# Cross attention on one core: in the first batch, Wv's sums and the next batch's A sums change places in VectorE's order

## Chip, core and metric

The kernel runs on one core of one Trainium2 chip. The metric is device time in microseconds (us). PE is the matrix engine, DVE the vector engine, ACT the scalar engine, POOL is GpSimd, and SP issues most transfers. "The trace" is one profiled execution of the kernel.

## What is computed

For eight batches, with x1 and x2 of 512 x 1024 (channels by positions), all in f32:

```python
q = jnp.einsum('bcn,dc->bnd', x1, Wq) + bq            # Wq 64 x 512
k = jnp.einsum('bcn,dc->bdn', x2, Wk) + bk[:, None]   # Wk 64 x 512
v = jnp.einsum('bcn,dc->bdn', x2, Wv) + bv[:, None]   # Wv 512 x 512
attn = jax.nn.softmax(jnp.einsum('bnd,bdm->bnm', q, k), axis=2)
attn_out = jnp.einsum('bcm,bnm->bcn', v, attn)
return attn_out + x1
```

## The kernel before

The product with v is reassociated: first y = x2 times the transposed attention (the "y" stage), then Wv times y (the "o" stage), plus bv and x1. Both are products of 2 x 2 blocks, and each is done with seven block products instead of eight (a Winograd form of Strassen's scheme). The left operand is A (x2 transposed, blocks "11" to "22") in the y stage and Wv (tiles `w`) in the o stage; its sums S1 to S4 are made by `left_sums`, four DVE instructions, of 128x1024 for A (through `sum_a`) and of 128x512 for Wv. The sum S3 is written over block 21. Wv's sums are made once, A's once per batch. The right operand, the exponentials e in the y stage and y in the o stage, has sums T1 to T4 (`sum_e`, `sum_y`).

The seven block products of a stage are numbered 1, 2, 6, 7, 5, 3, 4 as `multiply` knows them; the code's `first(i)` is a product of the y stage and `second(i)` one of the o stage. The y stage runs them in the order 1, 2, 6, 5, 7, 3, 4, with the next batch's scores before 5 and before 4; the o stage in the order 1, 6, 2, 5, 7, 3, 4 (the texts call these its stages). Products 1, 6, 5 and 3 accumulate in bank a, products 2, 7 and 4 in bank c; each bank has two halves (a0, a1; c0, c1), one per 128 rows. Products 1, 7 and 2 open a bank anew. After 1, 6 and 5 ACT copies the bank aside. The blocks of the result come out in the order 11, 22, 12, 21: 12 is read from bank a after product 3, the others from bank c.

Softmax runs on the scores transposed: `scores` (PE) and a copy to SBUF (ACT); `fold` takes the maximum over tiles (DVE); `highest` finishes it across partitions (POOL, tile `top`); `exponentials` subtracts it (DVE, L230) and exponentiates (ACT, L231). `sums` and `total` do the same with sums (tile `den`), and `shares` takes the reciprocal (DVE, L219).

The order is written out by hand. Each engine takes its instructions in the order of the code and stops at the first one whose inputs or buffers are not ready. `period(s, n, nn, nnn)` writes the work of batch s, and in between the scores and exponentials of the next batch n and the queries and keys of batches after it. `period` for s.b == 0 is the first batch. Lines to follow:

- L180 scores; the third tile of the second half goes to bank a (tile `ps_sa`), which `evict_y(s, "12")` (L306) must have emptied.
- L279 all block products of both stages (`ps_ya`, `ps_yc` for y; `ps_oa`, `ps_oc` for o).
- L308, L310 the evictions of y11, y22 and y21; L306 that of y12.
- L324, L331 the evictions of the result, `evict_o`; L332 their output transfers (SP).
- L100 the sums of `left_sums`, for A (`aS`, `a`) and for Wv (`w_S`, `w`).
- L201, L205 the folds; L210 and L215 POOL's reductions; L236 the T sums.
- L138 the projections of queries and keys (`ps_q`, `ps_k`).

Of the kernel before, what the change touches and what calls it, by code (L numbers as in the profile page):

```python
# [15 lines left out]
def kernel(  # L16
# [64 lines left out]
    w = {  # L81
        k: const.tile([P, 2, C // 2], F32, name=f"w_{k}")
        for k in ("11", "12", "21", "22", "S1", "S2", "S4")
    }
# [6 lines left out]
    def left_sums(a, *ks):  # L91

        for k in ks:
            x, y, op = {
                "S1": ("21", "22", ALU.add),
                "S2": ("S1", "11", ALU.subtract),
                "S3": ("11", "21", ALU.subtract),
                "S4": ("12", "S2", ALU.subtract),
            }[k]
            nc.vector.tensor_tensor(a["21" if k == "S3" else k], a[x], a[y], op)  # L100
            if k == "S3":
                a["S3"] = a["21"]
# [8 lines left out]
    def load_x(s, x):  # L111

        s.x = sb.tile([P, CT, N], F32, tag="x", name=f"x_{s.b}_{x.tensor.name}")
        for c in range(CT):
            nc.sync.dma_start(s.x[:, c, :], x[s.b, ts(c, P), :])

    def load_a(s, *ks):
        for k in ks:
            s.a[k] = sb.tile(
                [P, MH, C // 2], F32, tag=f"a{k}", name=f"a{k}_{s.b}", bufs=1 + (k[0] == "2")  # L120
            )
            nc.sync.dma_start(s.a[k], x2T[s.b, int(k[0]) - 1, int(k[1]) - 1])

    def sum_a(s, *ks):
        for k in ks:
            if k != "S3":
                s.a[k] = sb.tile([P, MH, C // 2], F32, tag=f"a{k}", name=f"a{k}_{s.b}")
        left_sums(s.a, *ks)
# [18 lines left out]
    def queries(s):  # L147

        ps = project(s, "q", wq_sb)
        s.q = sb.tile([P, N], F32, tag="q", name=f"q_{s.b}", bufs=2)  # L150
        for h, r, o in ((0, lo, hi), (1, hi, lo)):
            nc.scalar.activation(
                s.q[r, ts(h, H)], ps[r, :], AF.Identity, bias=bq_sb[r, :]
            )
        for h, r, o in ((0, lo, hi), (1, hi, lo)):
            nc.scalar.dma_start(s.q[o, ts(h, H)], s.q[r, ts(h, H)])

    def keys(s, bank=None):

        ps = project(s, "k", wk_sb, bank)  # L160
        s.k = sb.tile([P, H], F32, tag="k", name=f"k_{s.b}", bufs=2)
        nc.scalar.activation(s.k, ps, AF.Identity, bias=bk_sb)  # L162
# [49 lines left out]
    def total(s, h):  # L212
        fold_halves(s, h, ALU.add)
        s.den[h] = sb.tile([P, H], F32, tag="den", name=f"den_{s.b}_{h}", bufs=3)
        nc.gpsimd.partition_all_reduce(s.den[h], s.mx[h][:, 0, :], P, ReduceOp.add)  # L215

    def shares(s, h):
        s.rden[h] = s.den[h]
        nc.vector.reciprocal(s.rden[h], s.den[h])  # L219
# [18 lines left out]
    def open_t(s):  # L238
        for n in ("T1", "T2", "T4"):
            s.t[n] = sb.tile([P, MH, H], F32, tag=f"e{n}", name=f"e{n}_{s.b}")  # L240
        e0, e1 = s.e[0], s.e[1]
        s.t |= {"11": e0[:, 0], "12": e1[:, 0], "21": e0[:, 1], "22": e1[:, 1]}
        s.t["T3"] = s.t["12"]

    def sum_e(s, *ks):
        for i in (0, 2):
            part = {n: v[:, i : i + 2, :] for n, v in s.t.items()}
            for k in ks:
                right_sums(part, k)
# [19 lines left out]
    def multiply(s, stage, i, left, right, n_k):  # L269

        ka, kb, bank, opens = MULT[i]
        for j in range(2):
            if opens:
                s.bank[bank, j] = ps_a.tile(
                    [P, H], F32, tag=f"{bank}{j}", name=f"ps_{stage}{bank}{j}_{s.b}_{i}"
                )
            ps = s.bank[bank, j]
            for k in range(n_k):
                nc.tensor.matmul(  # L279
                    ps,  # L280
                    left[ka][:, k, ts(j, P)],
                    right[kb][:, k, :],
                    start=opens and k == 0,
                    stop=i in (2, 3, 4) and k == n_k - 1,
                    skip_group_check=True,
                )
            if i in (1, 6, 5):
                s.tmp[i, j] = sb.tile([P, H], F32, tag=f"u{i}{j}", name=f"u{stage}{i}{j}_{s.b}")
                nc.scalar.copy(s.tmp[i, j], ps)  # L289
# [29 lines left out]
    def evict_o(s, k):  # L319
        bank, add = RESULT[k]  # L320
        for j in range(2):
            c = 2 * (int(k[0]) - 1) + j
            o = s.o[k, j]
            nc.vector.scalar_tensor_tensor(  # L324
                o, s.bank[bank, j], bv_sb[:, c : c + 1], o, ALU.add, ALU.add
            )
        for j in range(2):
            c, h = 2 * (int(k[0]) - 1) + j, int(k[1]) - 1
            o = s.o[k, j]
            if add is not None:  # L330
                nc.vector.tensor_tensor(o, o, s.tmp[add, j], ALU.add)  # L331
            nc.sync.dma_start(out[s.b, ts(c, P), ts(h, H)], o)  # L332

    def sums(s, h):
        for i in range(1, MH):
            fold(s, h, i, "sum", ALU.add)
        total(s, h)
# [70 lines left out]
    def head_second(s, n):  # L408


        scores(s, 1, 3)()
        for i in range(2, MH):
            fold(s, 1, i, "max", ALU.max)
        queries(n)
        load_x(n, x2)
        highest(s, 1)
        sum_a(s, "S3", "S4")
        for i in range(MH):
            exponentials(s, 1, i)
# [11 lines left out]
    def period(s, n, nn, nnn):  # L431

        def first(i):
            multiply(s, "y", i, s.a, s.t, MH)

        def second(i):
            multiply(s, "o", i, w, s.y, 2)

        open_t(s)
        first(1)
        if s.b == 0:
            head_second(s, n)
        sum_e(s, "T1", "T2")
        if s.b == 0:
            total(s, 0)
        else:
            sum_e(s, "T4")
        if n:  # L450
            load_a(n, "11")
        first(2)
        if s.b == 0:
            keys(n)
            load_x(nn, x1)
            evict_y(s, "11", (1,))
            sum_e(s, "T4")
            shares(s, 0)
            evict_y(s, "11", (2,))
        else:  # L460
            shares(s, 0)
            evict_y(s, "11")
        sums(s, 1)
        sum_e(s, "T3")
        shares(s, 1)
        if n:
            load_a(n, "12", "21", "22")
        first(6)

        def next_queries():  # L470
            queries(nn)
            load_x(nn, x2)

        def next_keys():
            keys(nn)
            if nnn:
                load_x(nnn, x1)

        if n:
            scores_and(n, 0, "c", next_queries if nn else nothing)  # L480
            for i in range(1, MH):
                fold(n, 0, i, "max", ALU.max)
            highest(n, 0)
            if s.b == 0:
                left_sums(w, "S1", "S2", "S3", "S4")
        first(5)
        fetch_o(s, "11")
        fetch_o(s, "22")
        if n:
            for i in range(MH):  # L490
                exponentials(n, 0, i)
            if s.b:
                sum_a(n, "S1", "S2", "S3")
        first(7)
        evict_y(s, "22")
        first(3)
        evict_y(s, "12")
        if n:
            scores_and(n, 1, "a", next_keys if nn else nothing)
            sums(n, 0)  # L500
        sum_y(s, "T1")
        sum_y(s, "T2")
        if n:
            sum_a(n, *(("S4",) if s.b else ("S1", "S2", "S3", "S4")))
            for i in range(1, MH):
                fold(n, 1, i, "max", ALU.max)
            highest(n, 1)
        first(4)
        evict_y(s, "21")
        second(1)  # L510
        sum_y(s, "T3")
        sum_y(s, "T4")
        second(6)
        fetch_o(s, "12")
        if n:
            exponentials(n, 1, 0)
            exponentials(n, 1, 1)
        second(2)
        evict_o(s, "11")
        fetch_o(s, "21")  # L520
        second(5)
        if n:
            exponentials(n, 1, 2)
            exponentials(n, 1, 3)
        second(7)
        evict_o(s, "22")
        if n:
            second(3)
            evict_o(s, "12")
            second(4)  # L530
            evict_o(s, "21")
        else:
            second(4)
            evict_o(s, "21")
            second(3)
            evict_o(s, "12")
# [37 lines left out]
```

## Time and profile before

| | |
|---|---|
| median of 3 runs | 718.07 us (718.0 to 718.2) |
| the profiled execution | 718.06 us, of which the span is 716.0 us |
| PE busy | 706.1 us, 99% of the span |
| DVE busy | 590.9 us, 83% |
| ACT, POOL busy | 201.3 us (28%), 97.5 us (14%) |
| DMA | 87.39 MB, mean 122 GB/s |
| granted PE clock | 1.000 |

A busy PE is counted with overlapping instructions, so its share hides slow stretches; distances between the starts of stages show them. One batch follows another at 86.93 us once the kernel is under way (the first y product starts at 124.96 us in the second batch and at 211.89 us in the third). A wait of an engine is counted as idle time, with the instruction that ended it.

### The profile page before, as it was taken

To read this page: it belongs to the slowest core of one execution; us is meant where nothing else is said; L and a number is where in the kernel's file an instruction comes from. 1 tells how busy PE (TensorE), PEld (TensorE's weight loads), DVE (VectorE), ACT (ScalarE), POOL (GpSimd) and SP (SyncE) were. 2 spreads that over 40 slices of the span, in tenths; PEclk is the share of its full clock that TensorE was granted. 3 is DMA by queue.
4 is the path that set the end of the run, shared out by engine and by line. 5 is a ranking of instruction groups with operands and counts; after the bars stand their busy time and mean duration, and the time that the engine had idled before them with its cause. 6 is when DMAs were issued, how large, how long until landed. Compare 5 with 4: busy or idle time off the path is not lost.

```text
span 716.0 us, 5409 instructions
## 1 busy us (share of the span) xinstructions
PE 706.1 (99%) x1892; PEld 299.9 (42%) x1892; DVE 590.9 (83%) x569; ACT 201.3 (28%) x271; POOL 97.5 (14%) x38
## 2 busy tenths in 40 slices
PE   8999999999999999999999999999999999999997
PEld 4333334434444444444444443443434444444443
DVE  0999998988969888798887987889887898989444
ACT  2733313044210532215221232403324034230010
POOL 0132130030300311011200202002020020301000
PEclk9999999999999999999999999999999999999999
DMA  8577133341333503435133352332601350042004
GB/s 335 208 232 261 66 146 118 121 143 74 146 129 136 169 22 146 148 118 190 42 134 117 119 191 92 112 119 89 220 0 60 117 177 0 0 159 77 0 1 147
DMA packets 34699, 87.39 MB, mean 122 GB/s; under 512 B 3952, under 2 KB 3952, under 8 KB 34672
## 3 DMA queue, kind: packets, MB, share of 16 engines
q1 hardware_dynamic: 33344, 84.95, 33.8%
q10 hardware_dynamic: 1264, 2.10, 1.0%
q8 instruction: 15, 0.25, 0.1%
q14 instruction: 12, 0.10, 0.0%
q0 software_dynamic: 64, 0.00, 0.0%
HBM read 68.42 MB, written 16.78 MB: 119 GB/s over the span
## 4 chain that ended last, share of the span: by engine, by line
PE 85%; DVE 10%; DMA 2%; issue 1%; ACT 1%; SPq 0%; DVEq 0%; ACTq 0%
PE ps_ya L279 27%; PE ps_yc L279 20%; PE ps_oa L279 14%; PE ps_oc L279 12%; PE ps_s L180 5%; PE ps_k L138 3%; PE ps_q L138 3%; DVE max L201 2%; DMA a<-in_x2T_dram 1%; DVE e L230 1%; DVE eT L236 1%; DMA w<-in_wvT_dram 1%; DVE aS L100 1%; DVE den L219 1%; PE ps_sa L180 1%
## 5 line engine op out<-in xcount | busy, mean ns | idle before, releaser
L215 POOL PARTITION_ALL_REDUCE den<-sum x16 | 65.3, 4079 | 431.8 <-DVE sum L205 431.8
L279 PE MATMUL ps_ya<-eT,aS 128*128 128x512 f32 x256 | 113.1, 595 | 0.0
L279 PE MATMUL ps_yc<-e,a 128*128 128x512 f32 x256 | 112.6, 592 | 0.0
L289 ACT COPY uy<-ps_ya 128x512 f32<-128x512 f32 x48 | 28.1, 588 | 231.2 <-PE ps_ya L279 231.2
L230 DVE TENSOR_TENSOR e<-e,top 128x1024 f32<-128x1024 f32 x60 | 69.9, 1217 | 11.9 <-POOL top L210 11.9
L279 PEld LDWEIGHTS ps_ya<-eT,aS 128*128 128x128 f32 x256 | 48.0, 190 | 63.8 <-issue 63.5
L279 PEld LDWEIGHTS ps_yc<-e,a 128*128 128x128 f32 x256 | 48.6, 190 | 61.6 <-issue 60.1
L324 DVE SCALAR_TENSOR_TENSOR o<-ps_oc,bv_sb,o 128x512 f32<-128x512 f32 x48 | 35.8, 749 | 42.1 <-PE ps_oc L279 42.0
L231 ACT ACTIVATE e<-e 128x1024 f32<-128x1024 f32 x60 | 62.2, 1056 | 26.5 <-DVE e L230 24.7
L289 ACT COPY uo<-ps_oa 128x512 f32<-128x512 f32 x48 | 28.1, 585 | 131.0 <-PE ps_oa L279 127.7
L189 ACT COPY e<-ps_s 128x1024 f32<-128x1024 f32 x47 | 46.7, 1026 | 60.6 <-PE ps_s L180 60.6
L279 PE MATMUL ps_oc<-y,w 128*128 128x512 f32 x128 | 57.6, 593 | 0.3 <-DVE y L310 0.3
L279 PE MATMUL ps_oa<-yT,w_S 128*128 128x512 f32 x128 | 57.5, 592 | 0.0
L279 PE MATMUL ps_ya<-e,a 128*128 128x512 f32 x128 | 56.3, 593 | 0.8 <-ACT e L225 0.8
L279 PE MATMUL ps_yc<-eT,a 128*128 128x512 f32 x128 | 57.0, 598 | 0.0
L279 PE MATMUL ps_ya<-e,aS 128*128 128x512 f32 x128 | 56.2, 592 | 0.0
L219 DVE RECIPROCAL den<-den 128x512 f32<-128x512 f32 x16 | 53.6, 3348 | 0.0
L180 PE MATMUL ps_s<-q,k 64*128 64x512 f32 x188 | 47.9, 608 | 1.6 <-ACT k L162 0.8
L210 POOL PARTITION_ALL_REDUCE top<-max x16 | 30.6, 1913 | 133.6 <-DVE max L205 133.6
L308 DVE TENSOR_TENSOR y<-ps_yc,uy 128x512 f32<-128x512 f32 x48 | 31.2, 675 | 15.9 <-PE ps_yc L279 15.9
L201 DVE TENSOR_TENSOR max<-max,e 128x1024 f32<-128x1024 f32 x32 | 39.2, 1225 | 3.7 <-ACT e L187 0.5
L201 DVE TENSOR_TENSOR sum<-sum,e 128x1024 f32<-128x1024 f32 x32 | 39.2, 1225 | 2.1
(65 smaller groups left out, 758.6 us busy)
## 6 DMA issues: line engine op xcount, KB each, us to landing
x_in_x_dram<-in_x_dram SPq DMA_DIRECT2D x56, 512.0 KB, 5.6
a<-in_x2T_dram SPq DMA_DIRECT2D x32, 512.0 KB, 4.7
o<-in_x_dram SPq DMA_DIRECT2D x64, 256.0 KB, 6.4
out_dram<-o SPq DMA_DIRECT2D x64, 256.0 KB, 2.1
x_head<-in_x_dram SPq DMA_DIRECT2D x8, 512.0 KB, 8.0
q<-q ACTq DMA_DIRECT2D x14, 128.0 KB, 7.2
w<-in_wvT_dram SPq DMA_DIRECT2D x4, 256.0 KB, 8.9
wqk_sb<-in_wqk_dram ACTq DMA_DIRECT2D x1, 256.0 KB, 4.6
```

The source lines that it names most:

```text
L138: nc.tensor.matmul(ps[r, :], w_sb[:, c, :], s.x[:, c, ts(h, H)], start=(c == 0), stop=(c == CT - 1),)
L180: nc.tensor.matmul(ps[g], s.k[r, ts(i, P)], s.q[r, ts(h, H)], start=True, stop=True)
L189: nc.scalar.copy(e[:, :, i, :], whole)
L201: nc.vector.tensor_tensor(f, e[:, :, 0, :] if i == 1 else f, new, op)
L215: nc.gpsimd.partition_all_reduce(s.den[h], s.mx[h][:, 0, :], P, ReduceOp.add)
L219: nc.vector.reciprocal(s.rden[h], s.den[h])
L230: nc.vector.tensor_tensor(e, e, top, ALU.subtract)
L231: nc.scalar.activation(e, e, AF.Exp)
L279: nc.tensor.matmul(ps, left[ka][:, k, ts(j, P)], right[kb][:, k, :], start=opens and k == 0, stop=i in (2, 3, 4) and k == n_k - 1, skip_gr ...
L289: nc.scalar.copy(s.tmp[i, j], ps)
L308: nc.vector.tensor_tensor(y[:, j, :], ps, s.tmp[add, j], ALU.add)
L324: nc.vector.scalar_tensor_tensor(o, s.bank[bank, j], bv_sb[:, c : c + 1], o, ALU.add, ALU.add)
```

## The change

In the first batch only, two groups of DVE instructions get new places. The sums of Wv stood behind the maximum of the next batch's first half of scores; they now stand behind the sum T2 of y, where the next batch's A sums stood. Those A sums now stand behind the eviction of block 22 of the result, ahead of the evictions of 12 and 21. All other batches keep their order, and nothing is added or left out.

```diff
@@ -481,8 +481,6 @@
             for i in range(1, MH):
                 fold(n, 0, i, "max", ALU.max)
             highest(n, 0)
-            if s.b == 0:
-                left_sums(w, "S1", "S2", "S3", "S4")
         first(5)
         fetch_o(s, "11")
         fetch_o(s, "22")
@@ -501,7 +499,10 @@
         sum_y(s, "T1")
         sum_y(s, "T2")
         if n:
-            sum_a(n, *(("S4",) if s.b else ("S1", "S2", "S3", "S4")))
+            if s.b:
+                sum_a(n, "S4")
+            else:
+                left_sums(w, "S1", "S2", "S3", "S4")
             for i in range(1, MH):
                 fold(n, 1, i, "max", ALU.max)
             highest(n, 1)
@@ -524,6 +525,8 @@
             exponentials(n, 1, 3)
         second(7)
         evict_o(s, "22")
+        if s.b == 0:
+            sum_a(n, "S1", "S2", "S3", "S4")
         if n:
             second(3)
             evict_o(s, "12")
```

## The prediction

> **What bounds the kernel now.** I read the page's first part, then what PE waited for, then the timelines of PE, DVE and POOL through the first batch and the second beside it.
>
> ```profile
> span 716.0 us, 5409 instructions
> ...
> PE 706.1 (99%) x1892; PEld 299.9 (42%) x1892; DVE 590.9 (83%) x569; ACT 201.3 (28%) x271; POOL 97.5 (14%) x38
> ```
>
> PE is the bound almost throughout, so DVE work counts only where PE stands still for it. After the head of the kernel PE does that in two places, both in the first batch (columns: total us, times, longest us):
>
> ```profile
> PE ps_sa L180 <- DVE y L306: 1.4, 1, 1.4
> ...
> PE ps_oc L279 <- DVE y L310: 0.3, 1, 0.3
> ```
>
> The first is the third score tile of the second batch: it goes into bank a, which DVE has not yet emptied of y12. The second is stage 2 of the output, which needs y21. DVE's timeline shows what lay ahead of y12 (start, length):
>
> ```profile
> 75.74 0.69 DVE L205 TENSOR_TENSOR max<-max 128x512 f32<-128x512 f32 x1
> 76.35 0.69 DVE L100 TENSOR_TENSOR w_S<-w,w 128x512 f32<-128x512 f32 x1
> 77.07 1.41 DVE L100 TENSOR_TENSOR w_S<-w_S,w 128x512 f32<-128x512 f32 x1
> 78.41 0.68 DVE L100 TENSOR_TENSOR w<-w,w 128x512 f32<-128x512 f32 x1
> 79.01 0.68 DVE L100 TENSOR_TENSOR w_S<-w,w_S 128x512 f32<-128x512 f32 x1
> 79.61 4.62 DVE L230 TENSOR_TENSOR e<-e,top 128x1024 f32<-128x1024 f32 x4
> ...
> 86.55 1.27 DVE L306 TENSOR_TENSOR y<-ps_ya,den 128x512 f32<-128x512 f32 x2
> ```
>
> The four sums of Wv stand between the folded maximum and the exponentials, while POOL forms the maximum that the exponentials need. POOL's timeline, first batch and second:
>
> ```profile
> 76.61 2.07 POOL L210 PARTITION_ALL_REDUCE top<-max  x1 [8.03 <-DVE max L205]
> ...
> 157.47 1.78 POOL L210 PARTITION_ALL_REDUCE top<-max  x1 [8.02 <-DVE max L205]
> ```
>
> PE's timeline of the two batches gives the price of the waits, as distances between starts:
>
> ```profile
> 83.92 1.99 PE L180 MATMUL ps_s<-q,k 64*128 64x512 f32 x8
> ...
> 89.79 3.65 PE L138 MATMUL ps_k<-x_in_x_dram,wqk_sb 128*64 128x512 f32 x16
> ...
> 103.78 3.60 PE L279 MATMUL ps_oa<-yT,w_S 128*128 128x512 f32 x8
> 107.69 3.70 PE L279 MATMUL ps_oc<-y,w 128*128 128x512 f32 x8 [0.31 <-DVE y L310]
> ...
> 114.66 3.60 PE L279 MATMUL ps_oc<-y,w 128*128 128x512 f32 x8
> ...
> 124.96 7.03 PE L279 MATMUL ps_ya<-e,a 128*128 128x512 f32 x16
> ...
> 201.59 3.60 PE L279 MATMUL ps_oc<-y,w 128*128 128x512 f32 x8
> ```
>
> From the first score to the key projection takes 89.79 - 83.92 = 5.87 us here; in the second batch (173.67 to 177.30) it takes 3.63. So the wait costs 2.24 us, more than its 1.38 us of idle, because the second half of bank a is late too. From stage 6 to stage 7 takes 114.66 - 103.78 = 10.88; in the second batch (191.29 to 201.59) 10.30. That wait costs 0.58 us.
>
> **The change, part by part.** It only reorders eight DVE instructions. No operation, byte or DMA is added.
>
> *1. Wv's sums leave the place behind the maximum.* DVE gives back 79.61 - 76.35 = 3.26 us there, but the exponentials cannot start until POOL delivers the maximum. POOL starts at 76.61 and took 2.07 us with the sums beside it; in the second batch, with DVE idle, it took 1.78. The Trainium skill (SBUF — State Buffer, Who interferes with whom) says that a DVE instruction with two SBUF inputs contends with a GpSimd one that reads SBUF, and that whoever starts first holds the port for the whole instruction. The row of 1.41 us, a sum that otherwise takes 0.69, fits a collision, though not one held to the full 2.07. By the rule the reduction alone falls back to 1.78 and ends at 78.39; if its 2.07 is its own, it ends at 78.68. With the 0.04 us that DVE needs after it in the second batch (159.25 to 159.29) the exponentials start at 78.43 or 78.72, and DVE is 1.18 or 0.89 us earlier. I take 1.18: of the 16 maxima 13 have 1.78, and the three longer ones all have sums of DVE beside them.
>
> The y22 and y12 evictions follow straight behind, so bank a's halves come free 1.18 us earlier (the first at 86.06 instead of 87.24). PE cannot use them before 83.92 + 1.82 = 85.74, the distance that the second batch shows (173.67 to 175.49), so the whole 1.18 is on the path. About 1.06 of the 2.24 us stays lost. ACT's copies, which follow PE's scores by 1.17 us in the second batch, are not in the way.
>
> *2. Behind T2 of y, four sums of Wv stand in place of four sums of the next A.*
>
> ```profile
> 96.58 1.21 DVE L100 TENSOR_TENSOR aS<-a,a 128x1024 f32<-128x1024 f32 x1
> ...
> 101.24 1.22 DVE L201 TENSOR_TENSOR max<-e 128x1024 f32<-128x1024 f32 x1
> ```
>
> The A sums take 101.24 - 96.58 = 4.66 us. Those of Wv without the collision take 0.72 + 3 x 0.60 = 2.5 (the starts above; 0.72 where one needs the result just before it). DVE gains a further 2.1 and is then 3.3 us early; y21 is done about 3.3 us earlier, PE reaches it only 1.2 us earlier, and the 0.58 us of stage 2 goes. The sums' own users stay served: PE's stage 6 needs S2, due at about 96.7 against PE's 102.6; the others are needed later. Should one collide with POOL it costs 0.7 us more; y21's first half is due at 104.3 and PE wants it at 106.0, so 1.7 us of spare cover that, and I cost it at nothing. POOL's sum reduction (92.43 to 96.56, then 1.18 earlier) is over when they begin: T2 in front of them (3.15 us) ends with it.
>
> PE at stage 7 is then 1.18 + 0.58 = 1.76 us early: 112.90 instead of 114.66.
>
> *3. The A sums go behind the eviction of block 22.* Waiting behind them in DVE's queue are the evictions of 12 and 21, and in SP's queue their four output DMAs and the next load of A. The first product of the second batch needs bank a, which the eviction of 12 empties. From the second batch, where the end of stage 7 sets the pace:
>
> ```profile
> 207.09 0.74 DVE L324 SCALAR_TENSOR_TENSOR o<-ps_oa,bv_sb,o 128x512 f32<-128x512 f32 x1
> ...
> 211.89 7.03 PE L279 MATMUL ps_ya<-e,a 128*128 128x512 f32 x16
> ```
>
> Stage 7 starts at 201.59, so DVE reaches the eviction of 12 after 5.50 us and PE reaches the next batch after 10.30. Now 4.66 us of sums come between: the eviction starts after 10.16, its first half ends after 10.91 (0.75), and PE goes on 0.04 later (as from 87.24 to 87.28). So PE waits to 10.95 instead of 10.30: 0.65 us. The slack there, 10.30 - 5.50 - 0.75 - 0.04 = 4.01 us, covers most of the sums but not all. Bank a's second half is free 0.7 us later and needed 3.4 later.
>
> What is late next: the evictions of 12 and 21 take 1.33 + 1.33 + 1.20 = 3.86 us by their rows, so DVE begins the T sums of the second batch at 112.90 + 10.16 + 3.86 = 126.9 (127.03 now). PE is then 1.1 us early and DVE 0.1. They next meet at y11, where DVE now waits 0.99 us for PE at 138.96; that wait vanishes and nothing on PE moves. The SP queue holds no load that PE is near: the A load waits for PE's first product (131.82 now) with or without the change.
>
> Sum: -1.18 - 0.58 + 0.65 = -1.11 us; with about 0.05 for PE's restart (after the wait at 107.69 the next stage began 0.09 late) -1.06. From the second batch on no PE wait is recorded, so it reaches the end. The profiled execution took 718.06 us, 716.0 span and 2.06 around it, against the median 718.07: 718.07 - 1.06 = 717.0. Bounds: -1.3 if the bank wait is 0.4; -0.5 if the reduction stays at 2.07 and each A sum costs 0.06 more. The alternative by the port rule's absence alone is 0.29 higher, 717.3.
>
> **The rivals.**
>
> *The new wait does not form.* Then -1.76: 716.3, just over 0.2%. It needs the four sums done in 4.01 us, or bank a's first half free otherwise. For it: the margin is 0.65 us of 4.66, and PE's ends are modelled. Against it: DVE's queue is in order, the rows of the A sums hardly vary, and the last eviction of block 22 is tied to the end of stage 7, so DVE's earlier lead cannot be used. A milder form, a wait of 0.3, gives -1.4, at the 0.2% bound (1.44 us). 0.28 for more than 0.2%.
>
> *The A sums stall in their new place, and the second batch starts late.* Rows of collided A sums exist: the longest two took 1.94 and 2.06 us instead of 1.22. Four such take about 8.0 us, the wait at bank a becomes 4.0, and the balance is -1.76 + 4.0 = +2.2: 720.3. It decides from 1.76 + 4.01 = 5.8 us of sums to be slower at all, and from 7.2 to be slower by 0.2%. Against it: POOL has nothing between about 107.8 and 145.3, and both long rows lie beside a reduction in the head. 0.11, with unseen delays of that size at this place.
>
> *The first part does nothing*, because POOL or ACT holds the scores as late as before: then only 0.58 is gained and 0.65 lost, 718.1. The second batch, whose scores run without a wait, speaks against it. It lies within 0.2%.
>
> **How the numbers follow.** A measurement of this kernel can tell about 0.2% (1.44 us) from no change. My main case, -0.5 to -1.4, and the third rival lie within it: together 0.61. The range goes from the first rival, with 0.1 below it (716.2), to the third rival with 0.1 above (718.2); what is left out is nearly all of the slower case and a few hundredths of the others.
>
> **What would show it.** Right: POOL's reduction at 76.6 takes 1.78 us; the exponentials start at 78.4; PE waits for y12 0.3 to 0.5 us instead of 1.4; the wait for y21 is gone; a new PE wait of 0.5 to 0.8 us of ps_ya for the o of L324 near 123.8; the second batch's first product starts at 123.8 to 124.0. Wrong: that start at 123.2 (no wait), or after 125 (A sums stalled), or PE waits in the second batch, which I expect to have none.

## The result and the profile after

The changed kernel takes 717.1 us (median of 22 runs, 716.92 to 719.06), the kernel before 718.19 us in the same comparison (22 runs, 717.92 to 719.92). The ratio is 0.9986, 95% interval 0.998 to 0.9992: about 1.1 us, or 0.14%, faster, which lies within the 0.2% of the prediction. The forecast was 717.0 us.

PE's waits after (total us, times, longest us):

```profile
PE ps_ya L279 <- DVE o L324: 0.5, 1, 0.5
...
PE ps_sa L180 <- DVE y L306: 0.2, 1, 0.2
```

The wait for y12 fell from 1.4 to 0.2 us, the wait for y21 is gone, and there is one new wait: the first product of the second batch for the eviction of 12 (L324). DVE's timeline after (start, length):

```profile
75.58 0.69 DVE L205 TENSOR_TENSOR max<-max 128x512 f32<-128x512 f32 x1
78.26 4.63 DVE L230 TENSOR_TENSOR e<-e,top 128x1024 f32<-128x1024 f32 x4 [2.00 <-POOL top L210]
...
95.25 0.68 DVE L100 TENSOR_TENSOR w_S<-w,w 128x512 f32<-128x512 f32 x1
...
97.78 1.22 DVE L201 TENSOR_TENSOR max<-e 128x1024 f32<-128x1024 f32 x1
...
118.25 1.22 DVE L100 TENSOR_TENSOR aS<-a,a 128x1024 f32<-128x1024 f32 x1
...
122.92 1.40 DVE L324 SCALAR_TENSOR_TENSOR o<-ps_oa,bv_sb,o 128x512 f32<-128x512 f32 x2
```

This execution runs 0.16 us ahead of the one before already at the fold of 75.58 (75.74 before) and at the first score (83.76, 83.92 before). That arises at the head of the kernel, ahead of the first instruction that the change moves; distances between starts leave it out. From the fold to the exponentials DVE now takes 2.68 us instead of 3.87, and 2.00 of it is idle time that POOL ends. Wv's sums take 2.53 us behind T2, A's 4.67 us behind the eviction of 22. POOL's and PE's timelines after:

```profile
76.44 1.78 POOL L210 PARTITION_ALL_REDUCE top<-max  x1 [8.03 <-DVE max L205]
```

```profile
83.76 1.99 PE L180 MATMUL ps_s<-q,k 64*128 64x512 f32 x8
...
88.46 3.65 PE L138 MATMUL ps_k<-x_in_x_dram,wqk_sb 128*64 128x512 f32 x16
...
102.45 3.60 PE L279 MATMUL ps_oa<-yT,w_S 128*128 128x512 f32 x8
...
112.75 3.60 PE L279 MATMUL ps_oc<-y,w 128*128 128x512 f32 x8
...
123.72 7.13 PE L279 MATMUL ps_ya<-e,a 128*128 128x512 f32 x16 [0.51 <-DVE o L324]
130.69 7.03 PE L279 MATMUL ps_yc<-e,a 128*128 128x512 f32 x16
```

The reader can set up the whole balance from these starts. Scores to key projection: 88.46 - 83.76 = 4.70 us (5.87 before), so 1.17 won. Stage 6 to stage 7: 10.30 (10.88 before), 0.58 won. Stage 7 to the second batch: 10.97 (10.30 before), 0.67 lost. That makes 1.08 us up to the second batch. Its first product then takes 130.69 - 123.72 = 6.97 us to the next instead of 131.82 - 124.96 = 6.86, which costs 0.11 us more and leaves 0.97. The profiled spans differ by 1.1 us (716.0 and 714.9) because the 0.16 us of the head come on top; the medians differ by 1.09.

The distance from the scores hangs on when PE arrives there, and that varies with the head by some tenths of a us. From DVE's fold to the key projection it does not: 14.05 us in the two traces with the old order at this place (before, and the A sums alone below), 12.88 or 12.89 in the six with the new order and no other change ahead of it. The gain of 1.17 stands on that.

### The profile page after: what moved, and what is told of

Its sections match the earlier page's. It is cut to its first block, busy times and chain, and to the rows that moved or that the text cites. A ratio compares the mean times of both kernels' runs of the same rounds, so it can differ in the third digit from the quotient of the medians.

```text
span 714.9 us, 5407 instructions
## 1 busy us (share of the span) xinstructions
PE 705.6 (99%) x1892; PEld 299.8 (42%) x1892; DVE 590.2 (83%) x569; ACT 201.3 (28%) x271; POOL 97.2 (14%) x38
## 4 chain that ended last, share of the span: by engine, by line
PE 87%; DVE 8%; DMA 1%; issue 1%; ACT 1%; SPq 0%; POOL 0%; DVEq 0%; ACTq 0%; POOLq 0%
PE ps_ya L279 27%; PE ps_yc L279 21%; PE ps_oa L279 15%; PE ps_oc L279 11%; PE ps_s L180 5%; PE ps_k L138 3%; PE ps_q L138 3%; DVE max L201 1%; DMA x_head<-in_x_dram 1%; DVE eT L236 1%; DVE e L230 1%; DVE aS L100 1%; PE ps_sa L180 1%; DVE den L219 1%; PE ps_sc L180 1%
## 5 line engine op out<-in xcount | busy, mean ns | idle before, releaser
L324 DVE SCALAR_TENSOR_TENSOR o<-ps_oc,bv_sb,o 128x512 f32<-128x512 f32 x48 | 35.7, 749 | 41.6 <-PE ps_oc L279 41.5
```

Source lines behind the costliest of these rows:

```text
L324: nc.vector.scalar_tensor_tensor(o, s.bank[bank, j], bv_sb[:, c : c + 1], o, ALU.add, ALU.add)
```

## The experiments

**Each move alone.** First Wv's sums alone, against the kernel before:

```diff
-            if s.b == 0:
-                left_sums(w, "S1", "S2", "S3", "S4")
         first(5)
...
         if n:
+            if s.b == 0:
+                left_sums(w, "S1", "S2", "S3", "S4")
             sum_a(n, *(("S4",) if s.b else ("S1", "S2", "S3", "S4")))
```

> Only the first move: Wv's sums behind T2, the A sums stay where they were, behind them. Theory (PE pays where DVE is late): DVE gains 1.18 us at the scores (POOL's maximum, now 1.78 us, becomes the limit) but carries 2.53 us of Wv sums ahead of y21, so y21 is 1.35 later than before: PE's wait there grows, stage 2 of the output starts about 1.3 us later than before, and no PE wait forms at the start of the second batch. 718.2 + 1.3 = 719.5 us. Rival (the freed place alone brings the gain, the place behind T2 is free): 718.2 - 1.2 = 717.0.

Measured: 721.03 us, ratio 1.0043 (1.003 to 1.0055), 2.9 us slower than before. The direction is the theory's, the size twice it. PE's timeline and two stretches of the same trace (the last columns are granted clock, DMA share and GB/s):

```profile
109.19 5.40 PE L279 MATMUL ps_oc<-y,w 128*128 128x512 f32 x8 [2.85 <-DVE y L310]
114.42 1.02 PE L279 MATMUL ps_oa<-yT,w_S 128*128 128x512 f32 x2
```

```profile
109.00:111.00 2.00, 1.81 (x3) 0.79 (x4) 2.00 (x4) 0.21 (x1) 0.28 (x1) 0.59 0.00 0
111.00:113.00 2.00, 2.00 (x4) 0.86 (x3) 2.00 (x2) 0.00 (x0) 0.00 (x0) 0.55 0.03 8
```

Stage 2 starts at 109.19, 1.50 us later than before; 0.13 us of it is there already at the fold (75.87 against 75.74), and 1.37 remains against the theory's 1.35. But it then lasts 114.42 - 109.19 = 5.23 us to the next stage, against 3.53 before: after 2.85 us of idle the granted clock fell to about half (0.59 and 0.55 in the two stretches). The other 1.7 us are that. The rival is out: behind T2 Wv's sums cost time as long as the A sums stay there.

Then the A sums alone, against the kernel before:

```diff
-            sum_a(n, *(("S4",) if s.b else ("S1", "S2", "S3", "S4")))
+            if s.b:
+                sum_a(n, "S4")
...
         evict_o(s, "22")
+        if s.b == 0:
+            sum_a(n, "S1", "S2", "S3", "S4")
```

> Only the second move: the A sums behind the eviction of block 22, Wv's sums stay behind the maximum. Theory: the wait for y21 goes (-0.58), the wait for y12 stays at 1.4 us of idle and POOL's maximum at 2.07 us, and a new wait of PE for bank a at the start of the second batch costs 0.65 to 0.7. Together +0.1: 718.3 us. Rival (the A sums in the new place are hidden): 718.2 - 0.58 = 717.6.

Measured: 718.3 us, ratio 1.0003 (0.9994 to 1.0012). Stage 6 starts at 103.78 us, as before; then:

```profile
114.08 3.60 PE L279 MATMUL ps_oc<-y,w 128*128 128x512 f32 x8
...
125.04 7.13 PE L279 MATMUL ps_ya<-e,a 128*128 128x512 f32 x16 [0.50 <-DVE o L324]
```

The distances are 10.30 and 10.96, so 0.58 won and 0.66 lost, as the theory has it. The interval leaves the rival's 717.6 (0.9993 of 718.09) only just outside; the distances decide. As they were made here, the two moves only pay together: each alone gives nothing or a loss.

**How many sums fit behind the eviction of 22.** Three instead of four, with S4 one eviction later, against the changed kernel:

```diff
         if s.b == 0:
-            sum_a(n, "S1", "S2", "S3", "S4")
+            sum_a(n, "S1", "S2", "S3")
         if n:
             second(3)
             evict_o(s, "12")
+            if s.b == 0:
+                sum_a(n, "S4")
```

> As the changed kernel, but only S1, S2 and S3 of A behind the eviction of 22; S4 behind the eviction of 12. Theory: DVE has 4.01 us before PE needs bank a; three sums take 3.5 us and fit, so PE's wait for bank a goes and the second batch starts 10.30 us after stage 7 instead of 10.97: 717.1 - 0.67 = 716.4 us. Rival (the wait is not of the sums' length, or DVE's loss returns at y11 of the second batch): 717.1.

Measured: 716.45 us, ratio to before 0.9973 (0.9962 to 0.9983). PE's timeline shows the second batch following without a wait, 10.30 us after stage 7:

```profile
112.75 3.60 PE L279 MATMUL ps_oc<-y,w 128*128 128x512 f32 x8
...
123.05 7.03 PE L279 MATMUL ps_ya<-e,a 128*128 128x512 f32 x16
```

Five, six and seven sums, by computing S4 again with the same operands:

```diff
             sum_a(n, "S1", "S2", "S3", "S4")
+            left_sums(n.a, "S4")     # six: "S4", "S4"; seven: "S4", "S4", "S4"
```

> As the changed kernel, with S4 of A computed a second time behind the first (same operands, same result): five sums of A behind the eviction of 22. Theory: the slack is used up, so the whole of the fifth sum, 1.14 us from start to start, comes on top: second batch starts 12.1 us after stage 7, and DVE's arrival at y11 of the second batch, now without slack, shifts too but PE does not wait there: 717.1 + 1.14 = 718.2 us. Rival (the wait is fixed): 717.1.

> As the changed kernel, with S4 of A computed three times in all: six sums behind the eviction of 22; PE stands idle about 2.9 us before the second batch. Theory (after some 2.85 us of idle PE's granted clock fell to 0.50 in e1_wv_only, which cost 1.8 us on top of the wait): the start of the second batch 13.25 us after stage 7, then some 1.8 us more in its first product if the clock falls: 718.4 + 1.14 + 1.8 = 721.4. Rival (the idle alone counts): 719.6.

> As the changed kernel, with S4 of A computed four times in all: seven sums behind the eviction of 22; PE stands idle about 4.0 us. Theory (the clock falls): 719.6 + 1.14 + 1.8 or a little more = 722.6. Rival (the idle alone counts): 720.7.

Measured: 718.43, 721.29 and 723.27 us. PE's timeline with five:

```profile
124.98 7.13 PE L279 MATMUL ps_ya<-e,a 128*128 128x512 f32 x16 [1.76 <-DVE o L324]
```

Stage 7 starts at 112.75 as with four, so the second batch starts 12.23 us after it, at a granted clock of 1.00: 1.26 more than with four, 1.33 us in the medians of the two comparisons. The theory had 1.14; the repeated S4 writes the tile that was written just before, and starts 1.26 us behind it, about as S2 behind S1, whose result it needs (118.25 to 119.50 in the changed kernel's trace). With six the step is 2.9 us. PE's timeline with six, and a stretch of it:

```profile
126.30 8.56 PE L279 MATMUL ps_ya<-e,a 128*128 128x512 f32 x16 [3.02 <-DVE o L324]
134.70 6.60 PE L279 MATMUL ps_yc<-e,a 128*128 128x512 f32 x15
```

```profile
126.00:128.00 2.00, 1.70 (x2) 0.84 (x3) 2.00 (x4) 0.00 (x0) 0.00 (x0) 0.50 0.46 169
128.00:130.00 2.00, 2.00 (x5) 0.83 (x4) 2.00 (x4) 0.00 (x0) 0.00 (x0) 0.70 0.40 153
```

The product takes 8.40 us to the next instead of 6.97. With seven:

```profile
127.66 8.83 PE L279 MATMUL ps_ya<-e,a 128*128 128x512 f32 x16 [4.28 <-DVE o L324]
```

The next product starts at 136.33, 8.67 us later. The rival, that only the idle time counts, is out for both; it had 719.6 and 720.7. The theory, 721.4 and 722.6, is met with six and 0.7 us short with seven.

**The gap in which DVE waits for POOL.** Two of Wv's sums back in it, against the changed kernel:

```diff
             highest(n, 0)
+            if s.b == 0:
+                left_sums(w, "S1", "S2")
...
-                left_sums(w, "S1", "S2", "S3", "S4")
+                left_sums(w, "S3", "S4")
```

> As the changed kernel, but two of Wv's sums (S1, S2) stay in the gap behind the maximum, where DVE only waits for POOL; S3 and S4 are behind T2. Theory (sums with two SBUF inputs beside POOL's reduction lengthen it): the reduction takes about 2.07 us instead of 1.78, S2 about 1.4 instead of 0.69, the exponentials start 0.29 later, and the kernel is 0.3 us slower than the changed one: 717.4. Rival (the gap is free, two sums of 0.69 fit into 2.0 us): 1.78 us and 717.1.

Measured: 717.43 us, ratio to before 0.999 (0.9981 to 0.9999), 0.3 above the changed kernel's 717.1 from the other comparison (0.4 by the differences to the kernel before). The profiled execution is one of the two long ones of this run (718.81), but the excess lies ahead of the fold. The timelines of POOL and DVE decide:

```profile
78.06 2.07 POOL L210 PARTITION_ALL_REDUCE top<-max  x1 [8.03 <-DVE max L205]
```

```profile
77.19 0.69 DVE L205 TENSOR_TENSOR max<-max 128x512 f32<-128x512 f32 x1
77.80 0.69 DVE L100 TENSOR_TENSOR w_S<-w,w 128x512 f32<-128x512 f32 x1
78.52 1.41 DVE L100 TENSOR_TENSOR w_S<-w_S,w 128x512 f32<-128x512 f32 x1
80.16 4.63 DVE L230 TENSOR_TENSOR e<-e,top 128x1024 f32<-128x1024 f32 x4 [0.23 <-POOL top L210]
```

The reduction is back at 2.07 us and S2 at 1.41, and the fold-to-exponentials distance is 2.97 us (77.19 to 80.16) against 2.68. From the fold to the key projection (90.35) it is 13.16 us against 12.88. So the two do slow each other, and the price to the path is 0.28 us here.

**What is left at the scores.** On top of the three-sum version, the fourth exponential tile goes behind the copies of the scores:

```diff
-            for i in range(MH):
+            for i in range(MH if s.b else MH - 1):
                 exponentials(n, 0, i)
...
+        def last_and_keys():
+            if s.b == 0:
+                exponentials(n, 0, MH - 1)
+            next_keys()
...
-            scores_and(n, 1, "a", next_keys if nn else nothing)
+            scores_and(n, 1, "a", last_and_keys if nn else nothing)
```

> As e3, and in the first batch the fourth exponential tile of the next batch's first half goes behind the copies of the scores, so that y22 and y12 are evicted 1.14 us earlier. Theory (the loss left at the scores, 88.46 - 83.76 = 4.70 us against 3.63 in the second batch, is y12 being late): it vanishes, 716.45 - 1.07 = 715.4 us; DVE is back on its course at the sums. Rival (PE is then held by ACT's copies of the scores, or the late exponential delays y21): 716.4 or more.

Measured: 715.41 us, ratio to before 0.9961 (0.9947 to 0.9974), 2.7 us faster than before and, across the two comparisons, about 1.6 faster than the changed kernel: the best version tried. All its runs (715.22 to 715.66) lie below all those of the three-sum version (716.16 to 716.63). PE's timeline:

```profile
84.27 1.99 PE L180 MATMUL ps_s<-q,k 64*128 64x512 f32 x8
...
87.90 3.65 PE L138 MATMUL ps_k<-x_in_x_dram,wqk_sb 128*64 128x512 f32 x16
```

87.90 - 84.27 = 3.63 us, exactly the second batch's distance. The late tile costs DVE 1.23 us of waiting for ACT further on, and y21 still comes almost in time: stage 6 to stage 7 takes 10.36 us (101.89 to 112.25) instead of 10.30. In this trace PE arrives at the scores 0.30 us later than in that of the three-sum version (84.27, 83.97), so the key projection starts only 0.56 us earlier (87.90, 88.46); the 1.04 us rest on the medians.

## Why the prediction was right

Its three terms, in its order:

- *Scores, -1.18.* Measured -1.17. The choice inside it was to let POOL's reduction fall back to 1.78 us rather than keep 2.07. It did, and putting two sums back restored 2.07 and 1.41. The port rule that the prediction took from the Trainium skill (SBUF — State Buffer, Who interferes with whom) points the right way, but the numbers are milder than a port held for a whole instruction: S2 was stretched by 0.72 us and the reduction by 0.29, not one by the other's full length. That it is the port, and not any work of DVE beside POOL, no run here separates. The statement that 1.06 us would stay lost agrees with the last experiment, which won 1.04 in the median.
- *Stage 2, -0.58.* Measured -0.58, alone (A sums only) and together.
- *The wait for bank a, +0.65.* Measured +0.67. The slack of 4.01 us was read from the second batch, and the counts of three and five sums bracket it: three sums cost nothing, four cost 0.67, and a fifth shows with its whole 1.26 us.
- *DVE afterwards.* The T sums of the second batch begin at 126.75; with the head's 0.16 us added that is 126.91, and 126.9 was forecast. The 0.99 us wait at y11 is gone, and no PE wait is recorded in later batches.

Three things in it were off. PE's restart was put at about 0.05 us and cost 0.11; by the distances the balance is -0.97 where -1.06 was forecast, so the agreement of the medians (-1.09) is closer than the working. PE's idle time for y12 was to be 0.3 to 0.5 us; by the prediction's own numbers, 1.38 - 1.18, it should have said 0.2, and 0.2 was measured, but the traces with the same order up to there show from none to 0.41, as PE arrives later or earlier, so this sign decides little. And the rival "slower" assumed that a wait costs its own length. That holds to 1.76 us of idle: its point of no gain, 5.8 us of sums, is met by five sums (5.93 us, ratio 1.0003). Beyond it fails: six sums take 7.18 us, for which the rule gives 0.2% more time, and cost 0.44%, because the clock fell as well. A stall of the rival's size would have cost more than its sum says: it had 720.3 us for about 8.0 us of sums, and seven sums, 8.45 us, took 723.27.

Of the other rivals, "the new wait does not form" was priced at 716.3; the version in which it does not form took 716.45.

## What to carry to other kernels

Where one engine is the bound and takes its work in order, price a reordering at the few instructions where that engine stands still: find how much slack each place has from a later, undisturbed repetition of the same code, and compare it with the length of the moved group. Moving a group can need its partner to move too: each half of this change alone brought nothing or lost. A group that just misses its slack is better split than moved whole, and the instructions that stay should be looked at for what still stands between the bound engine and the buffer it needs.

## What was not expected of the hardware

PE's clock answers to waits of a few microseconds. After 2.85, 3.02 and 4.28 us of idle (one trace each) the granted clock went to 0.50 just before or soon after PE resumed, and the work behind took 1.70, 1.43 and 1.70 us longer; after 1.76 us, and after the 1.38 us of the kernel before, it stayed at 1.00.

The traces say how long. The clock is at 0.50 from 109.37 to 112.79 us (Wv's sums alone), 125.80 to 129.21 (six sums) and 128.68 to 132.09 (seven), each time 3.4 us. Half speed for that long costs 1.7 us, as measured twice; with six sums PE resumed only at 126.30, so 2.91 us of slow work remain, worth 1.46, and 1.43 was measured. The Trainium skill (TensorE: Matmul & The Clock Gate, Part 1) has the array fall to half its clock after at least one idle window of about 3.4 us that runs freely, and recover after about as long of work. The length agrees, and so does the moment of the fall, which is 2.5 to 5.3 us after PE stopped. But the window need not be wholly idle: of the 3.41 us that ended where the clock fell, PE stood idle for 2.85, 2.52 and 2.39 us. In the 3.42 us before those, the trace with seven sums has 1.89 us of idle, and the clock stayed at 1.00. So by this estimate, from three gaps and with modelled ends of PE's work, the fall needs somewhere between 1.89 and 2.39 us of idle in one such window, and a gap of a given length can be cheap or dear by where the window falls. No run here moved a gap on purpose to test that.
